# Forward transforms of a graph's tokens from three overlapping blocks of 104 instead of two blocks of 128, and the first filter tiles loaded earlier

## The chip, the cores and the metric

One core of a Trainium2 chip runs the whole program. The metric is the device time of one launch in microseconds (us): the median of three runs of the kernel before is 2039.37 us (2038.85 to 2040.94). Beside these there is one profiled execution, from which all durations below are taken.

The engines are named as in the profile: PE is the matrix engine's matmul side and PEld its weight loads, DVE the vector engine, ACT the scalar engine, POOL the general engine, SP the engine whose queue issues nearly all DMAs.

## The reference, cut to what matters

The input is 64 graphs of 256 nodes (tokens) with 256 features and a 256 x 256 adjacency matrix each, all float32. Two layers follow each other:

```python
# layer 0
h = relu(layernorm(x))
x = x + relu(norm_adj @ h @ W.T + b)
# layer 1
h = relu(layernorm(x))
c = relu(bn1(conv1(h)))              # 1 tap
c = bn2(conv2(c))                    # 17 taps over the tokens, padding 8
x_conv = relu(c + h)
s   = h @ w_se.T + b_se              # 3 columns
A   = exp(-dist(s, s)) * adj
nmp = A @ relu(h @ w_msg.T + b_msg)
gi, gh = [x_conv, nmp] @ w_ih.T + b_ih, h @ w_hh.T + b_hh
r, z = sigmoid(gi_r + gh_r), sigmoid(gi_z + gh_z)
x = x + (1 - z) * tanh(gi_n + r * gh_n) + z * h
```

The change lies in `conv2`, the convolution of 17 taps.

## The kernel before, in words

**The convolution by transforms.** The 256 tokens of a graph are cut into 8 windows. Window `w` has 48 tokens, begins 8 tokens ahead of token 32*w, and yields 32 outputs. Each window is taken to 48 real spectral numbers (`W48`), each spectral number is multiplied by a 256 x 256 filter, and the result is taken back. The 64 graphs go through this in four groups (`GROUPS`) of 16 graphs (`NG`), so that 16 x 8 = 128 windows stand side by side in the tile `Xf` (128 partitions, 48 spectral numbers, two halves of 128 channels, 128 windows).

**The forward transform.** `spectrum(g, cb)` takes one graph and one half of its channels. The graph's tokens lie in the tile `h1l` with tokens on the partitions, as two blocks of 128 tokens. For each block there is one matmul with 128 x 128 of `h1l` as weights and a constant table `dft` as the moving operand. Block 0 holds tokens of windows 0 to 4 and block 1 of windows 3 to 7, so each matmul has 48 x 5 = 240 columns and the two add up in windows 3 and 4. On PE each float32 matmul of the program is two instructions with a weight load each. One `spectrum` is therefore four matmul instructions. Then `act.copy` takes the 384 columns from PSUM into `Xf`.

```python
for nb in range(NB):
    pe.matmul(t[:, :, 3 * nb : 3 * nb + 5], h1[:, nb, cb * P : (cb + 1) * P], dft[:, nb],
              start=(nb == 0), stop=(nb == NB - 1), skip_group_check=True)
```

**Where the tokens come from.** `conv1` writes each graph's `c1o` to a scratch in device memory, `h1d`, as it lies in the tile (each partition's two rows of 1 KB next to each other, 2 KB), and `h1_load` brings it back into `h1l`. There are three buffers of `h1l` (`H1 = 3`): when the second half of graph g is done, the load for graph g + 3 is issued from SP's queue.

**The products.** `product(u)` multiplies spectral unit u (24 of them) by its filters. The filters come from the scratch `wfd` in 71 parts of 256 KB, through six buffers `wf` (`WF = 6`): `wf_load(n)` loads part n, and each part's use issues the load of the part six further on.

**The order of the work.** The first stage computes layer 0, `conv1` and the messages for all graphs, in a loop over `n`; the group 0 of the convolution (16 x 2 calls of `spectrum`, then 24 of `product`) is dealt out between its matmuls. Then comes, for q = 1, 2, 3, a stage of its own with the 32 calls of `spectrum` of group q back to back, here called the spectrum stage of group q; after it the loop over the 16 graphs of group q - 1 calls `gates`, with the products of group q dealt out between the gates of the first four graphs. At q = 4 only gates are left. PE, ACT, DVE and POOL instructions of this part keep the order in which they are written; `after(beats, go)` puts off a step by so many calls of `beat`, and `Paced` deals out the inverse transforms by the time that `beat` is told. In the spectrum stage each `spectrum` ends with `cv.beat(0.81)`.

In the stage of group q the first six filter parts are loaded at its last six graphs: `if g >= NG - WF: wf_load(g - NG + WF)`.

Of the kernel before, what the change touches and what calls it, by code (L numbers as in the profile page):

```python
# [11 lines left out]
FP = mybir.dt.float32  # L12
# [15 lines left out]
W48 = 48  # L28
OUT = 32
# [7 lines left out]
    return 2.0 * np.pi * f / W48  # L37


def dft_table():  # L40


    tab = np.zeros((128, 2, W48, 5), np.float64)
    p = np.arange(128)
    for b in range(2):
        for k in range(5):
            w = 128 * b + p - (OUT * (3 * b + k) - 8)
            inside = (w >= 0) & (w < W48)
            tab[:, b, 0, k] = inside / 48.0
            tab[:, b, 1, k] = inside * (1.0 - 2.0 * (w % 2)) / 48.0  # L50
            for u, f in enumerate(CPLX, 1):
                a = turn_of(f) * (w % W48)
                tab[:, b, 2 * u, k] = inside * np.cos(a) / 24.0
                tab[:, b, 2 * u + 1, k] = inside * -np.sin(a) / 24.0
    return tab.astype(np.float32)


def filter_table():
# [127 lines left out]
def gnn_kernel(  # L186
# [9 lines left out]
    nc = tc.nc  # L196
    B, N, D = x.shape
    P = 128
    KW = conv2_w.shape[2]
    NB = N // P  # L200
# [3 lines left out]
    NG = 16  # L204
    WT = N // OUT
    GROUPS = B // NG
# [4 lines left out]
    def scratch(name, shape):  # L211
        return dram.tile(shape, FP, tag=name, name=name)
# [2 lines left out]
    h2_d = [scratch(f"h2d_{q}", [NG * N, D]) for q in range(GROUPS)]  # L215
    hT_d = [scratch(f"hTd_{g}", [P, DC * N]) for g in range(B)]
    xn_d = [scratch(f"xnd_{g}", [P, DC * N]) for g in range(B)]
    h1_d = [scratch(f"h1d_{g}", [P, NB * D]) for g in range(B)]

    wt_d = scratch("wtd", [KW, D, D])  # L220
    wf_d = scratch("wfd", [3 * UNITS, D, D])
# [12 lines left out]
    brzB = const.tile([P, 2 * D], FP, tag="brzB", name="brzB")  # L234
    bnB = const.tile([P, 2 * D], FP, tag="bnB", name="bnB")

    dft = const.tile([P, 2, W48, 5], FP, tag="dft", name="dft")

# [33 lines left out]
    H1 = 3  # L274
# [10 lines left out]
    def conv_begin(q):  # L285
        cv.q = q
        cv.free = [[Z(cv.scr, 2 * k), Z(cv.scr, 2 * k + 2)] for k in (2, 4)]
        cv.G, cv.A, cv.y, cv.at = {}, {}, {}, {}

    def h1_load(q, g):  # L290
        h1 = cv.stream.tile([P, NB, D], FP, tag="h1l", name=f"h1l_{q}_{g}", bufs=H1)
        cv.dma.dma_start(h1, h1_d[q * NG + g].rearrange("p (c d) -> p c d", c=NB))
        cv.h1[q, g] = h1

    def spectrum(g, cb):

        q, Xf, h1 = cv.q, cv.Xf, cv.h1[cv.q, g]
        t = cv.bank(f"df_{q}_{g}_{cb}")[:, : W48 * WT].rearrange("p (s w) -> p s w", s=W48)
        for nb in range(NB):
            pe.matmul(  # L300
                t[:, :, 3 * nb : 3 * nb + 5], h1[:, nb, cb * P : (cb + 1) * P], dft[:, nb],
                start=(nb == 0), stop=(nb == NB - 1), skip_group_check=True,
            )
        if cb == DC - 1:
            del cv.h1[q, g]
            if g + H1 < NG:
                h1_load(q, g + H1)
        after(0, lambda: act.copy(Xf[:, :, cb, g * WT : (g + 1) * WT], t))
        cv.beat(0.81)

    def sums(u):

# [8 lines left out]
    def wf_load(n):  # L321
        if n < len(PARTS):
            u, k = PARTS[n]
            cv.wf[n] = wf = cv.stream.tile(
                [P, DC, D], FP, tag="wf", name=f"wf_{cv.q}_{u}_{k}", bufs=WF
            )
            cv.dma.dma_start(wf, wf_d[3 * u + k].rearrange("(c p) d -> p c d", c=DC))
# [236 lines left out]
    with ExitStack() as one:  # L564
# [483 lines left out]
        def conv1(g):  # L1048
            t = to_rows(g, "c1", w1T)

            def keep():
                h1 = work.tile([P, NB, D], FP, tag="c1", name=f"c1o_{g}")
                act.activation(h1, t, AF.Relu)
                nc.sync.dma_start(h1_d[g].rearrange("p (c d) -> p c d", c=NB), h1)
            after(1, keep)
            if g + 1 < B:
                after(2, lambda: own_bank("c1", g + 1, b1B))
# [244 lines left out]
        begin()  # L1302
        for n in range(4, B + 5):
            even, odd = n % G == 0, n % G == 1
            if n == B + 1:
                early_stack.close()
                kept()
                for g in range(H1):
                    h1_load(1, g)
            elif n == B + 2:  # L1310
                paced.do(4, outputs_out)
            if filtering and not items:
                filtering.clear()
                while due:
                    beat(0.0)
                conv_start()
            if n == B - 2:

                share[:] = 0.45, 0.6, 0.33
            elif n == B:  # L1320
                share[:] = 0.65, 0.75, 0.4
            if even and n + 2 * G < B:
                load(n + 2 * G)
            if n <= B + 1:
                turn_h(n - 2)
            beat(0.4)
            item()
            if n < B:
                aggregate(n)
                if odd and n + 1 < B:  # L1330
                    after(2, lambda n=n: factors(n + 1))
                    for r in range(NR):
                        after((5, 7, 8, 9)[r], lambda r=r, n=n: layer0_in(n + 1, (r,)))
                if even and n < B - G:
                    for r in (0, 2):
                        after(1 + r // 2, lambda r=r, n=n: row_moments(n + G, (r, r + 1)))
                if even and n + G < B:
                    after(4, lambda n=n: degrees(n + G))
            beat(1.7)
            item()  # L1340
            if even and n <= B + 2:
                turn_cols(n - 4)
            beat(0.2)
            if n + 1 < B:
                turn_adj(n + 1)
            beat(0.4)
            item()
            if n >= 5:
                pass_messages(n - 5)
            beat(1.7)  # L1350
            item(True)
            if n <= B + 1:
                messages(n - 2)
            beat(1.7)
            item()
            if even and n <= B + 2:
                distance(n - 4)
            beat(0.6)
            item()
            if n < B:  # L1360
                project(n)
            beat(1.7)
            item(True)
            if n <= B:
                conv1(n - 2)
            elif n == B + 2:
                conv1(B - 1)
            beat(1.7)
            item()
            if later:  # L1370
                for go in later.pop(0):
                    go()
                if not later:
                    while due:
                        beat(0.0)
                    prep_stack.close()
                    spec_stack = ExitStack()
                    spec = spec_stack.enter_context(tc.tile_pool(name="spec", bufs=1))
                    tab = spec.tile([P, 3 * UNITS], FP, tag="tab", name="tab")
                    nc.sync.dma_start(tab, nc.inline_tensor(filter_table(), name="tab_c").ap())  # L1380
                    tp = {k: filter_load(k) for k in range(2)}
                    filtering.append(True)
                    pace[:] = FILTER / 2, -7.0
                    items.extend(
                        lambda k=k, j=j: filter_part(k, j) for k in range(4) for j in range(QC // 8)
                    )
# [249 lines left out]
    for q in range(1, GROUPS + 1):  # L1636
        share[:] = 0.6, 0.6, 0.3
        ld = gate_inputs(q - 1, 0)
        paced.drain()
        outputs_out()  # L1640
        paced.drain()
        cv.taken = 0
        if q == 1:
            gate_weights()
        first = dict(zip((1, 3, 5, 6), gate_parts(ld, xcT)))
        todo = []
        if q < GROUPS:
            conv_begin(q)
            for g in range(NG):
                if g >= NG - WF:  # L1650
                    wf_load(g - NG + WF)
                for cb in range(DC):
                    spectrum(g, cb)
                if g in first:
                    first.pop(g)()
            while paced.lines[2]:
                beat(0.2)
            for u in range(1, AHEAD):
                sums(u)
            todo = [lambda u=u: product(u) for u in range(UNITS)]  # L1660
        for go in first.values():
            go()
        for g in range(NG):
            share[:] = (0.44, 0.58, 0.3) if todo else (0.53, 0.66, 0.3)
            lead = [todo.pop(0) for _ in range(LEAD if todo and g == 0 else 0)]
            between = [todo.pop(0) if todo else lambda: None for _ in range(PER)]
            ahead, nxt = None, None
            if g + 1 < NG:
                ahead = gate_inputs(q - 1, g + 1)
                nxt = gate_parts(ahead, xcT)  # L1670
            gates(ld, lead, between, nxt)
            ld = ahead
            if q + 1 < GROUPS and g >= NG - H1:
                h1_load(q + 1, g - NG + H1)
    while due:
# [33 lines left out]
```

## Time and profile before

| | |
|---|---|
| median of three runs | 2039.37 us (2038.85 to 2040.94) |
| the profiled execution | 2038.4 us, of which 2036.6 us from its first to its last instruction |
| granted clock of PE | 0.997 |
| busy: PE, PEld, DVE, ACT, POOL | 98%, 85%, 69%, 50%, 54% |
| `df` matmuls (the forward transforms) | 512 instructions, 111.6 us busy |
| spectrum stages of groups 1, 2, 3 | from 837.9, 1158.5 and 1479.2 us, some 28 us each |
| forward transforms of group 0 | between 370 and 474 us, among other matmuls |
| DMA queue that SP feeds | 329.62 MB, 51.3% of the 16 DMA engines' time |

How to read it: a group's line gives the line of the program, the engine, the operation, the tile it writes and those it reads, the shape, the number of instructions; then the busy time in us and the mean ns of one; then the idle time of the engine just ahead of them and what ended it. Nearly all instructions carry L102, the line of a helper that records them, so groups are told apart by tiles. Matmuls are pipelined: an instruction's own duration is longer than its step to the next one. In the timeline a row gives the start, the length, the engine, the group and a count, and in brackets the idle time ahead of it with its releaser.

### The profile page before, as it was taken

What the parts mean: (1) busy time and instruction counts of PE and PEld (TensorE: products, weight loads), DVE (VectorE), ACT (ScalarE), POOL (GpSimd) and SP (SyncE); (2) the same over time, 40 slices, a digit from 0 to 9 for tenths busy, and PEclk for the clock granted to TensorE, in tenths of its full rate; (3) what the DMA queues carried; (4) which work ended last, traced back from release to release, by engine and by line L of the source; (5) the groups of instructions that cost most, each with busy time, mean ns of one, the idle gap of its engine ahead of it and who ended that gap; (6) DMA issues with size and microseconds to landing.
All of it is one profiled execution on the core that took longest, in us unless ns stands there. A gap on an engine that the chain in (4) does not pass through costs nothing. (4 is left out here: it accounts for less than half of the span.)

```text
span 2036.6 us, 33041 instructions
## 1 busy us (share of the span) xinstructions
PE 1998.3 (98%) x10857; PEld 1738.0 (85%) x10857; DVE 1402.9 (69%) x3182; ACT 1013.4 (50%) x2203; POOL 1104.6 (54%) x1298
## 2 busy tenths in 40 slices
PE   7999999999999999899999999999999999999998
PEld 6877777888998888799888899888889988888887
DVE  5657666544488888337999825999924999965555
ACT  5757666665446777523344532344443244443333
POOL 4333333334775554358666528676627776655544
PEclk9999999999999999999999999999999999999999
DMA  8797887656755553666223366433266532223222
GB/s 287 253 249 258 242 254 249 226 168 221 241 182 191 169 175 139 209 194 205 93 94 100 111 209 197 125 99 95 93 195 205 155 99 89 93 86 101 93 88 73
DMA packets 283279, 336.17 MB, mean 165 GB/s; under 512 B 18499, under 2 KB 231126, under 8 KB 282454
## 3 DMA queue, kind: packets, MB, share of 16 engines
q1 hardware_dynamic: 282822, 329.62, 51.3%
q0 software_dynamic: 288, 4.46, 0.6%
q8 instruction: 87, 1.43, 0.3%
q14 instruction: 82, 0.67, 0.1%
HBM read 207.65 MB, written 126.35 MB: 164 GB/s over the span
## 5 line engine op out<-in xcount | busy, mean ns | idle before, releaser
L102 PE MATMUL n<-wiT,hx 128*128 128x256 f32 x1024 | 241.9, 379 | 0.0
L102 PEld LDWEIGHTS n<-wiT,hx 128*128 128x128 f32 x1024 | 194.6, 190 | 26.5
L102 DVE SCALAR_TENSOR_TENSOR Xf<-Xf 128x256 f32<-128x256 f32 (+1 forms) x248 | 182.6, 755 | 14.0 <-ACT Xf L102 10.3
L102 PEld LDWEIGHTS y<-Xf,wf 128*128 128x128 f32 x1536 | 184.7, 192 | 8.2 <-PE tc L102 2.8
L102 PE MATMUL y<-Xf,wf 128*128 128x128 f32 x1536 | 186.7, 275 | 3.1 <-issue 3.1
L102 PE MATMUL ta<-T,S 128*128 128x256 f32 x768 | 186.8, 379 | 1.7 <-ACT p L102 1.7
L102 POOL TENSOR_TENSOR rs<-ve,mhalf 128x2 f32<-128x2 f32 x65 | 52.2, 803 | 230.9 <-DVE nm L102 229.8
L102 PEld LDWEIGHTS ta<-T,S 128*128 128x128 f32 x768 | 144.2, 190 | 20.8 <-ACT p L102 2.1
L102 POOL TENSOR_TENSOR rz<-u,p 128x256 f32<-128x256 f32 x64 | 48.7, 761 | 201.9 <-ACT u L102 187.3
L102 DVE TENSOR_TENSOR Xf<-y,k 128x256 f32<-128x256 f32 x184 | 69.3, 418 | 127.1 <-PE y L102 99.1
L102 POOL TENSOR_TENSOR xs<-Xf 128x256 f32<-128x256 f32 x92 | 70.3, 770 | 151.2 <-PE y L102 103.1
L102 ACT ACTIVATE rz<-rz 128x512 f32<-128x512 f32 x128 | 80.1, 626 | 120.7 <-DVE rz L102 112.7
L102 DVE SCALAR_TENSOR_TENSOR h2l<-rz,h2l 128x256 f32<-128x256 f32 x128 | 107.3, 839 | 44.4 <-POOL h2l L102 44.4
L102 POOL TENSOR_TENSOR aT<-e,adjT 128x512 f32<-128x512 f32 x62 | 83.4, 1362 | 99.5 <-ACT e L102 95.6
L102 POOL TENSOR_TENSOR Xf<-Xf 128x256 f32<-128x256 f32 (+2 forms) x136 | 130.2, 963 | 3.4 <-DVE Xf L102 1.4
L102 ACT COPY k<-y 128x512 f32<-128x512 f32 x92 | 53.9, 586 | 156.7 <-PE y L102 156.7
L102 PE MATMUL n<-whT,hx 128*128 128x256 f32 x512 | 131.4, 379 | 0.0
L102 PE MATMUL ms<-wmT,h2T 128*128 128x259 f32 x512 | 126.6, 390 | 4.4 <-ACT h2T L102 4.4
L102 POOL TENSOR_TENSOR adjH<-adjT,eye 128x512 f32<-128x512 f32 x63 | 82.4, 1307 | 85.4 <-ACT adjT L102 84.1
L102 PE MATMUL ag<-adjH,hs 128*128 128x256 f32 x512 | 124.0, 384 | 3.2 <-ACT hs L102 2.3
L102 PE MATMUL nm<-aT,mso 128*128 128x256 f32 x512 | 122.1, 382 | 4.8 <-DVE pre L102 3.5
L102 PE MATMUL o<-w0T,aggT 128*128 128x256 f32 x512 | 124.0, 385 | 1.1 <-ACT e L102 1.1
(178 smaller groups left out, 5032.6 us busy)
## 6 DMA issues: line engine op xcount, KB each, us to landing
wf<-wfd SPq DMA_DIRECT2D x284, 256.0 KB
wfd<-fo SPq DMA_DIRECT2D x32, 576.0 KB
x2d<-x SPq DMA_DIRECT2D x64, 256.0 KB
h2d<-h SPq DMA_DIRECT2D x64, 256.0 KB
hTd<-h2T SPq DMA_DIRECT2D x64, 256.0 KB
h1d<-c1o SPq DMA_DIRECT2D x64, 256.0 KB
xnd<-xnT SPq DMA_DIRECT2D x64, 256.0 KB
h1l<-h1d SPq DMA_DIRECT2D x64, 256.0 KB
```

What stands on the lines that cost most here:

```text
L102: return self.tc.keep_in_program_order(getattr(self.engine, op)(*args, **kwargs))
```

## The change

The tokens of a graph are read as three blocks of 104 tokens that begin at tokens 0, 76 and 152. Block 0 holds the windows 0 to 2 whole, block 1 the windows 3 and 4, block 2 the windows 5 to 7. Each half of a graph takes three matmuls with 144, 96 and 144 columns, none of which adds to another. `h1d` now has one row of 1 KB for each token; it is stored as such, and `h1_load` reads 104 partitions x 3 rows of 1 KB out of it with steps that overlap (312 KB instead of 256 KB). The table `dft` has 384 columns instead of 480. `beat` is told 0.71 instead of 0.81. The first six filter parts of group 1 are loaded in the first stage (`n == B - 2`; that queue is ordered by a scheduler, which puts them right behind the last filter loads of group 0), and those of groups 2 and 3 one each behind the gates of graphs 8 to 13 of the group before.

```diff
+CHUNK, SHIFT = 104, 76
+SPANS = ((0, 3), (3, 5), (5, 8))
...
-    h1_d = [scratch(f"h1d_{g}", [P, NB * D]) for g in range(B)]
+    h1_d = [scratch(f"h1d_{g}", [N, D]) for g in range(B)]
...
-    dft = const.tile([P, 2, W48, 5], FP, tag="dft", name="dft")
+    dft = const.tile([P, W48 * WT], FP, tag="dft", name="dft")
...
+    def overlapped(rows):
+        return bass.AP(
+            tensor=rows.tensor, offset=rows.offset,
+            ap=[[D, CHUNK], [SHIFT * D, len(SPANS)], [1, D]],
+        )
     def h1_load(q, g):
-        h1 = cv.stream.tile([P, NB, D], FP, tag="h1l", name=f"h1l_{q}_{g}", bufs=H1)
-        cv.dma.dma_start(h1, h1_d[q * NG + g].rearrange("p (c d) -> p c d", c=NB))
+        h1 = cv.stream.tile([P, len(SPANS), D], FP, tag="h1l", name=f"h1l_{q}_{g}", bufs=H1)
+        cv.dma.dma_start(h1[:CHUNK], overlapped(h1_d[q * NG + g]))
...
-        for nb in range(NB):
+        for c, (w0, w1) in enumerate(SPANS):
             pe.matmul(
-                t[:, :, 3 * nb : 3 * nb + 5], h1[:, nb, cb * P : (cb + 1) * P], dft[:, nb],
-                start=(nb == 0), stop=(nb == NB - 1), skip_group_check=True,
+                t[:, :, w0:w1], h1[:CHUNK, c, cb * P : (cb + 1) * P],
+                dft[:CHUNK, W48 * w0 : W48 * w1].rearrange("p (s w) -> p s w", s=W48),
+                start=True, stop=True, skip_group_check=True,
             )
...
-        cv.beat(0.81)
+        cv.beat(0.71)
...
-                nc.sync.dma_start(h1_d[g].rearrange("p (c d) -> p c d", c=NB), h1)
+                nc.sync.dma_start(h1_d[g].rearrange("(c p) d -> p c d", p=P), h1)
...
+            if n == B - 2:
+                for k in range(WF):
+                    wf_load(k)
...
-                if g >= NG - WF:
-                    wf_load(g - NG + WF)
...
+            if q + 1 < GROUPS and 8 <= g < 8 + WF:
+                wf_load(g - 8)
```

More of the change, by code (lines that the diff above doesn't have):

```diff
@@ L37, in turn_of @@
     return 2.0 * np.pi * f / W48
+CHUNK, SHIFT = 104, 76
+SPANS = ((0, 3), (3, 5), (5, 8))
 def dft_table():
-    tab = np.zeros((128, 2, W48, 5), np.float64)
+    tabs = []
     p = np.arange(128)
[L45 to L50, printed above, removed]
+    for c, (w0, w1) in enumerate(SPANS):
+        tab = np.zeros((128, W48, w1 - w0), np.float64)
+        for k in range(w1 - w0):
+            w = SHIFT * c + p - (OUT * (w0 + k) - 8)
+            inside = (w >= 0) & (w < W48) & (p < CHUNK)
+            tab[:, 0, k] = inside / 48.0
+            tab[:, 1, k] = inside * (1.0 - 2.0 * (w % 2)) / 48.0
             for u, f in enumerate(CPLX, 1):
                 a = turn_of(f) * (w % W48)
-                tab[:, b, 2 * u, k] = inside * np.cos(a) / 24.0
-                tab[:, b, 2 * u + 1, k] = inside * -np.sin(a) / 24.0
-    return tab.astype(np.float32)
+                tab[:, 2 * u, k] = inside * np.cos(a) / 24.0
+                tab[:, 2 * u + 1, k] = inside * -np.sin(a) / 24.0
+        tabs.append(tab.reshape(128, -1))
+    return np.concatenate(tabs, 1).astype(np.float32)
 def filter_table():
@@ L298, in spectrum @@
         t = cv.bank(f"df_{q}_{g}_{cb}")[:, : W48 * WT].rearrange("p (s w) -> p s w", s=W48)
-        for nb in range(NB):
+        for c, (w0, w1) in enumerate(SPANS):
             pe.matmul(
-                t[:, :, 3 * nb : 3 * nb + 5], h1[:, nb, cb * P : (cb + 1) * P], dft[:, nb],
-                start=(nb == 0), stop=(nb == NB - 1), skip_group_check=True,
+                t[:, :, w0:w1], h1[:CHUNK, c, cb * P : (cb + 1) * P],
+                dft[:CHUNK, W48 * w0 : W48 * w1].rearrange("p (s w) -> p s w", s=W48),
+                start=True, stop=True, skip_group_check=True,
             )
```

## The prediction

> **What bounds the kernel now.** I read the page first, then the groups by form, then timelines of the stages that the change touches, and last the DMA semaphores in the trace.
>
> ```profile
> span 2036.6 us, 33041 instructions
> PE 1998.3 (98%) x10857; PEld 1738.0 (85%) x10857; DVE 1402.9 (69%) x3182; ACT 1013.4 (50%) x2203; POOL 1104.6 (54%) x1298
> ```
>
> PE is busy throughout; what shortens PE's stream shortens the span where nothing else becomes late. The groups give the work that is changed:
>
> ```profile
> L102 PE MATMUL y<-Xf,wf 128*128 128x128 f32 x1536 | 186.7, 275 | 3.1 <-issue 3.1
> L102 PE MATMUL df<-dft,h1l 128*128 128x240 f32 x512 | 111.6, 368 | 4.0 <-DMA h1l<-h1d 3.1 <-ACT Xf L102 0.9
> L102 ACT COPY Xf<-df 128x384 f32<-128x384 f32 x128 | 60.9, 480 | 40.9 <-PE df L102 40.3
> ```
>
> The `df` matmuls already waited 3.1 us for `h1l`, the load that the change makes larger. PE's timelines give the steps (first in group 0, then in the stage of group 1, then a product):
>
> ```profile
> 370.00 0.97 PE L102 MATMUL df<-dft,h1l 128*128 128x240 f32 x4
> 370.81 1.89 PE L102 MATMUL o<-w0T,aggT 128*128 128x256 f32 x8
> ...
> 854.75 5.63 PE L102 MATMUL df<-dft,h1l 128*128 128x240 f32 x27
> 860.80 2.77 PE L102 MATMUL df<-dft,h1l 128*128 128x240 f32 x12 [0.42 <-DMA h1l<-h1d]
> ...
> 882.15 1.95 PE L102 MATMUL y<-Xf,wf 128*128 128x128 f32 x16
> ```
>
> A row's length less one matmul's own duration, over the steps in it: 240 columns take (5.63 - 0.37) / 26 = 202.5 ns, 256 columns (1.89 - 0.38) / 7 = 216, 128 columns with a weight load for each (1.95 - 0.275) / 15 = 111.7. The line through the first two is 0.84 ns a column and 1.5 ns: 144 columns would take 122 ns, 96 columns 82.
>
> **The matmuls.** Each half of a graph had four steps of 202.5 ns, 810 ns. Now it has four of 122 and two of 96 columns. No row shows a matmul so short. Its lower end is the line, 82 ns. The upper end is the product row, 112 ns: there each step carries a weight load of 128 columns, and 128 columns by the line would be 109, so the load, not the matmul, seems to end the step. The trace has two loads of `df` that nothing held apart, at 860.773 and 860.882 us: 109 ns. I take 112, since a load must fit beside each short matmul: 4 x 122 + 2 x 112 = 712 ns, or 98 ns saved a half (158 ns at the lower end). A graph takes 1.42 us instead of 1.62.
>
> The Trainium skill bears against the change here: "TensorE: Matmul & The Clock Gate", section "LDWEIGHTS (loading the stationary operand)", says that a weight load's time goes by its columns over 1.2 and not by its rows, so 104 rows would load no faster than 128. By it the short step would be about 107 ns, an estimate, and the half 702 ns.
>
> **Group 0.** Between 370 and 474 us the `df` matmuls stand among others with PE busy all the time (the windows give 104.00 of 104.00 us), a graph passes every 6.5 us, so a slower load is hidden. 32 halves x 98 ns = 3.1 us gained (5.1 at the other end).
>
> **The load.** In the stages of groups 1 to 3 the load for graph g + 3 is issued when graph g is done and must have landed two graphs later: 2 x 1.62 = 3.24 us before, 2 x 1.42 = 2.84 after. What must fit: in the trace PE's next graph began at 856.98 and SP issued at 857.18 (0.20); the load landed 3.49 us after its issue, at 860.67; the next weight load began at 860.77 (0.10), and the restart cost another 0.10. Sum 3.89, less 3.24 is 0.65 lost, and the matmul starts show just that. So the chain is 0.40 us plus the landing time.
>
> Undisturbed, the semaphores show landing times of 2.5 to 2.8 us, say 2.6. A load of 128 partitions raises its semaphore by 16 separate landings: 16 engines with 8 packets of 2 KB (median 84 ns). The number of engines goes by partitions: the 72-partition stores `wfd<-fo` show one raise 0.48 us after the issue, before data can have landed, and then 12; a 3-partition load shows one and 3. So 104 = 8 x 13 partitions should go to 13 engines, with 8 x 3 = 24 packets of 1 KB (median 46 ns, mean 52). Transfer 24 x 46 = 1.10 us against 8 x 84 = 0.67: 0.43 later, 3.03 us. The filter loads, 16 packets of 1 KB an engine, landed at best in 2.52, and 8 packets more make 2.9. Ends: 2.8 (19.5 packets on 16 engines) and 3.4 (the excess of the means under load). Chain 3.43 against 2.84: about 0.59 lost, once in three graphs, because three buffers go round together. A graph in the load-bound rhythm costs 1.42 + 0.20 = 1.62, as before: in these stages the wait takes back most of what PE gains.
>
> The skill's "DMA: Bandwidth & Descriptors", section "Why a DMA increments its semaphore by 16 and not by 1", has a rule for it: the largest number up to 16 that divides the slowest dimension. It gives 13 too, so the sum by it is the same; but the page's section "Rules for kernel authors" asks for a multiple of 16 there, which speaks against blocks of 104.
>
> **Group 1's stage** now runs from 837.89 to 865.85. SP is held by the `hx` loads until 840.29, and the first `h1l` load behind them landed at 843.81. With 0.43 more graph 3 starts at 844.37, later than the 843.95 before: the first three graphs gain nothing. With 0.1 for the restart and 13 graphs x 1.42 = 18.5 it would end at 862.9; four waits of 0.59 make 865.3. Gain 0.5. Before, the filter loads in the last six graphs put 0.9 us into the loads' landing (3.5 us each of the last three); that is gone.
>
> **Groups 2 and 3** open with another wait:
>
> ```profile
> 1160.44 0.47 ACT L102 COPY Xf<-df 128x384 f32<-128x384 f32 x1
> 1161.77 0.42 ACT L102 ACTIVATE nn<-u 128x256 f32<-128x256 f32 x1 [0.86 <-DVE u L102]
> 1162.09 0.58 ACT L102 COPY n<-bnB 128x512 f32<-128x512 f32 x1
> 1162.61 1.23 ACT L102 COPY Xf<-df 128x384 f32<-128x384 f32 x3
> ...
> 1163.13 7.56 PE L102 MATMUL df<-dft,h1l 128*128 128x240 f32 x36 [0.45 <-ACT Xf L102]
> ```
>
> ACT is held by the last gates' chain, three PSUM banks are full, and PE stands after 2.5 graphs until 1163.13. ACT's and DVE's order is the same in both programs, so this time stays. From it 13.5 graphs x 1.42 = 19.2, four waits 2.4, 0.1 restart and 0.2 for a load that meets the output store make 1185.0 against 1186.6: 1.6 gained. Group 3, from 1483.89 to 1507.13, likewise 1.4.
>
> **The filter loads.** In the compared order of SP's queue, group 1's six follow group 0's last one among the stores of `h1d`, `hTd` and `h2d`, ahead of `xnd`. They wait for the products to release `wf`; by PE's timeline the last such matmuls end at 599.9 us, `xnd` was issued at 602.41: nothing behind them is late. If it were, a store would slip by up to 4 us, and its tile has two buffers. The other twelve wait for nothing (the products end at graph 3) and cost SP 0.36 us each, while the DMA engines are 30% busy; `hx` is needed a whole graph later. The first product waited for no DMA before, so earlier filters bring nothing there. The `h1d` stores have twice the packets of half the time: nothing. ACT copies at 480 ns fit into 712, and the smaller beat reorders one POOL subtraction.
>
> **The sum.** 3.1 + 0.5 + 1.6 + 1.4 = 6.6 us. The profiled execution took 2038.4 us, the median 2039.37 is 1.0 above it; so 2031.8 and, for the median, 2032.7.
>
> **Rivals.** *The load stays hidden*: chain at or under 2.84, landing under 2.45. The 13 waits (three stages of four, and group 1's graph 3) of about 0.59 would be gone: 7.5 more, 2025.2. Against it: no load landed under 2.47 even with 16 KB an engine. Chance 0.15. *Loaded packets*: the landing time rises to 3.6, as the last three loads of a stage showed, at every load; 13 x 0.57 = 7.4 is lost again and the time is about 2040. The 13 engines would be 78% busy (1.10 of 1.42 us) where 16 were 41% busy (0.67 of 1.62). Chance 0.15. *Slower, by the number of engines*: if the load went to 8 engines, 104 = 8 x 13, an engine would have 39 packets, 39 x 52 = 2.0 us a graph and a stage 3 x 1.42 + 13 x 2.0 = 30.3 against 28.0; three times 2.3 less 3.1 is 3.8 lost, 2043.2, and more with waits on top. It decides from 1.9 us a load upwards. The 72-partition store, on 12 engines and not 8 or 9, speaks against. Chance 0.08.
>
> **The numbers.** My forecast has 0.62, with its own range 2029 to 2036.5 by landing times of 2.8 to 3.3. 0.2%, about what a measurement of this kernel can tell from no change, is 4.1 us, so faster means under 2035.3: 0.55 of the forecast and the hidden case, 0.70. Same: the forecast's upper end 0.07, most of the loaded case 0.13, 0.20. Slower: 0.10. The range 2026.5 to 2038.5 leaves out the 8 engines, half the loaded case and part of the hidden one.
>
> **What would show it.** Right: `df` steps of 122 and 112 ns, 712 ns a half, in group 0 without waits; in the stages a wait of PE for `h1l` of some 0.6 us every third graph, 24 packets of 1 KB an engine and 13 landings a load, stages of about 27.4, 26.5 and 26.5 us. Wrong: stages near 23 us (the load hidden), steps of 82 ns, or stages over 28 us.

## The result, and the profile after

The changed kernel takes 2045.28 us (median, 2043.07 to 2056.19) where the kernel before takes 2039.87 us (2036.39 to 2042.85) on the same chips, 20 runs each. The ratio is 1.0035 with a 95% interval of 1.0025 to 1.0045: 5.4 us slower by the medians and 7 us by the ratio, where 6.6 us faster was forecast. The profiled execution took 2047.6 us, at a mean granted clock of 0.992 against 0.997 before.

The head of its page (the first two lines) and the groups of the forward transforms, from the groups by form (busy us, mean ns, then PE's idle time ahead of them and what ended it):

```profile
span 2045.8 us, 33539 instructions
PE 1998.9 (98%) x11113; PEld 1742.9 (85%) x11113; DVE 1401.8 (69%) x3182; ACT 1012.7 (50%) x2203; POOL 1104.4 (54%) x1298
```

```profile
L108 PE MATMUL df<-dft,h1l 104*128 104x144 f32 x512 | 106.0, 314 | 12.6 <-DMA h1l<-h1d 8.5 <-ACT Xf L108 3.7
...
L108 PE MATMUL df<-dft,h1l 104*128 104x96 f32 x256 | 48.4, 273 | 0.0
```

PE is as busy as before, 1998.9 against 1998.3 us, though it has a fifth fewer `df` columns, and the span is 9.2 us longer. The busy times of the two groups overlap and do not add up. Together the `df` matmuls keep PE busy for 111.5 us, as long as before (111.6), where the kernel without the loads, shown below, needs 97.9 us for the same ones: their durations stretch when the clock falls. The wait for `h1l` has grown from 3.1 to 8.5 us. The windows show where the time went (stages of groups 1, 2 and 3, then the first stage's part with group 0; columns as the first line tells), first for the kernel before, then for the changed one:

```profile
core 0: us, PE busy (x) PEld busy (x) DVE busy (x) ACT busy (x) POOL busy (x), PEclk, DMA share, GB/s
837.90:865.90 28.00, 26.66 (x133) 24.22 (x130) 1.56 (x2) 16.82 (x36) 11.57 (x15) 1.00 0.69 209
1158.40:1186.60 28.20, 26.73 (x131) 24.06 (x129) 7.42 (x18) 16.33 (x35) 5.30 (x6) 1.00 0.63 193
1479.20:1507.20 28.00, 26.77 (x130) 24.11 (x130) 7.38 (x18) 16.33 (x35) 5.28 (x6) 1.00 0.65 194
370.00:473.80 103.80, 103.80 (x545) 90.92 (x544) 51.19 (x172) 66.77 (x141) 35.02 (x45) 1.00 0.59 193
```

```profile
core 0: us, PE busy (x) PEld busy (x) DVE busy (x) ACT busy (x) POOL busy (x), PEclk, DMA share, GB/s
835.60:869.50 33.90, 30.01 (x197) 28.43 (x194) 1.11 (x2) 16.84 (x36) 11.60 (x15) 0.85 0.57 160
1162.00:1191.50 29.50, 24.93 (x195) 23.39 (x194) 7.45 (x18) 16.33 (x35) 5.33 (x6) 1.00 0.61 173
1484.10:1516.40 32.30, 28.16 (x194) 26.63 (x193) 7.39 (x18) 16.33 (x35) 5.27 (x6) 0.89 0.56 158
369.40:470.50 101.10, 101.10 (x610) 90.00 (x609) 51.16 (x172) 65.78 (x141) 34.80 (x45) 1.00 0.65 210
```

From the starts of PE's instructions the stages take 33.8, 29.4 and 32.3 us against 28.0, 28.1 and 27.9 before: 11.5 us lost. The part of group 0 takes 101.0 against 103.8: 2.8 us gained. The remaining 0.5 us up to the 9.2 lies ahead of and between these parts. PE's timeline of the stage of group 1:

```profile
835.62 4.67 PE L108 MATMUL df<-dft,h1l 104*128 104x144 f32 x36
842.50 15.45 PE L108 MATMUL df<-dft,h1l 104*128 104x144 f32 x84 [2.20 <-DMA h1l<-h1d]
858.94 1.67 PE L108 MATMUL df<-dft,h1l 104*128 104x144 f32 x12 [1.00 <-DMA h1l<-h1d]
860.78 6.75 PE L108 MATMUL df<-dft,h1l 104*128 104x144 f32 x48 [0.17 <-DMA h1l<-h1d]
867.93 1.67 PE L108 MATMUL df<-dft,h1l 104*128 104x144 f32 x12 [0.40 <-DMA h1l<-h1d]
```

The first three graphs (36 instructions) pass in 4.4 us, then PE stands 2.20 us. After that 84 instructions take 15.45 us, 184 ns each instead of some 120. Two things are seen here: PE waits for the load, and a stretch runs slowly. The windows of the two stretches of the stages with the lowest granted clock (same columns) tell why:

```profile
844.20:854.40 10.20, 10.20 (x44) 10.20 (x45) 1.11 (x2) 4.01 (x9) 4.73 (x6) 0.50 0.40 109
1496.10:1502.90 6.80, 6.80 (x32) 6.80 (x31) 0.00 (x0) 2.08 (x5) 0.00 (x0) 0.50 0.51 127
```

PE's clock was granted at half, 0.50, for 10.2 and 6.8 us. The steps there are 240 ns for 144 columns. The kernel before has no such stretch between 151 and 2035 us. The changed kernel has one more, 3.4 us from 823.7 us, ahead of the stages and behind a wait of PE for DVE; the kernel without the loads, shown below, has it too, so it does not come from them.

### The profile page after: what moved, and what is told of

It reads as the page before. It is cut to its first block, busy times and chain, and to the rows that moved or that the text cites. A ratio compares the mean times of both kernels' runs of the same rounds, so it can differ in the third digit from the quotient of the medians.

```text
span 2045.8 us, 33539 instructions
## 1 busy us (share of the span) xinstructions
PE 1998.9 (98%) x11113; PEld 1742.9 (85%) x11113; DVE 1401.8 (69%) x3182; ACT 1012.7 (50%) x2203; POOL 1104.4 (54%) x1298
```

## The experiments

Two theories were set against each other. Theory A: the `h1l` load lands too late for three buffers, PE waits, and the waits bring the clock down. The rivals: the moved filter loads cost time elsewhere (B), the new matmuls are slow in themselves (C), the size of the load or of its rows counts (D, E). Ratios below are against the kernel before on the same chip, with 95% intervals; times are medians.

### The filter loads alone, and the change without them

`wf_alone` is the kernel before with this edit only; `wf_back` is the changed kernel with it undone:

```diff
+            if n == B - 2:
+                for k in range(WF):
+                    wf_load(k)
...
-                if g >= NG - WF:
-                    wf_load(g - NG + WF)
...
+            if q + 1 < GROUPS and 8 <= g < 8 + WF:
+                wf_load(g - 8)
```

> The kernel before with the filter loads moved as in the change, transforms as before. Theory A (late h1l loads and the clock that drops while PE waits make the loss): the last three h1l loads of a stage land 2.6 us after issue instead of 3.5, some 0.7 us a stage, so 2 to 2.5 us faster than before, about 2037.5. Theory B (the moved filter loads cost time elsewhere): 3 us or more slower than before.

> The changed kernel with the filter loads back in the last six graphs of the stage. Theory A: the loads meet the h1l loads, which land later still, 1 to 3 us a stage: 2047 to 2052. Theory B: the loss goes away, 2040 or less.

`wf_alone`: 2038.14 us, 0.9984 (0.9975 to 0.9993). Its stages take 27.3, 27.1 and 27.2 us. `wf_back`: 2059.21 us, 1.0099 (1.0080 to 1.0117), with stages of 35.3, 38.7 and 32.0 us and half clock for 27 us; the loss is larger than expected. Moving the filter loads is therefore a gain of 0.16% by itself and saves the changed kernel some 14 us. Theory B falls.

### The load taken away

`no_load` leaves out the loads of graphs 3 to 15 of each group:

```diff
-    def h1_load(q, g):
+    def h1_load(q, g, old=None):
+        if old is not None:
+            cv.h1[q, g] = old
+            return
...
-                h1_load(q, g + H1)
+                h1_load(q, g + H1, h1)
```

> The changed kernel without the h1l loads of graphs 3 to 15 of each group: these graphs take the tokens of earlier ones, so the output is another; all else as in the change. It takes away the wait for the load alone. Theory A (the load's lateness is the whole loss): stages of 23 to 24 us, no half clock, 2023 to 2027. Theory C (the shorter matmuls are slow or wait for something else): stages stay at 26 us or more, above 2032.

2024.34 us, 0.9919 (0.9903 to 0.9934). PE's timeline of its stage of group 1, and the windows of the three stages (columns as above):

```profile
835.80 23.22 PE L108 MATMUL df<-dft,h1l 104*128 104x144 f32 x192
```

```profile
835.80:858.90 23.10, 23.10 (x197) 23.03 (x194) 1.53 (x2) 16.72 (x36) 12.29 (x15) 1.00 0.18 53
1151.40:1175.50 24.10, 23.15 (x194) 22.91 (x193) 7.53 (x18) 16.32 (x35) 5.42 (x6) 1.00 0.13 42
1468.10:1492.20 24.10, 23.14 (x194) 22.90 (x194) 7.42 (x18) 16.33 (x35) 5.29 (x6) 1.00 0.12 39
```

All 192 instructions of the stage of group 1 run without a gap, 23.05 us for 32 halves, 720 ns each, at full clock. The stages of groups 2 and 3 take 24.05 us each, with a single wait of some 0.95 us, for ACT. So nothing is wrong with the matmuls (C falls), and the loads cost the changed kernel 2045.28 - 2024.34 = 20.9 us by the medians, and 1.16% or some 24 us by the ratios. In the profiled executions the loss lies in the stages alone: the three together differ by 24.4 us, the spans by 24.0.

### More buffers, or a larger block

`h1_4` has `H1 = 4`. `c112` has other blocks, which also hold the windows whole, and 112 = 7 x 16 partitions; `c128` likewise with 128. `c112_h4` has both.

```diff
-    H1 = 3
+    H1 = 4
```

```diff
-CHUNK, SHIFT = 104, 76
+CHUNK, SHIFT = 112, 72      # c112, c112_h4;  128, 64 in c128
```

> The changed kernel with four buffers of h1l instead of three: a load has three graphs, 3 x 1.42 = 4.27 us, from issue to use. Theory A: chain 0.4 + 3.3 to 3.9, nearly all waits go and the clock stays up: stages of 23 to 25 us instead of 29 to 34, 2023 to 2029. Theory C: the stages stay as long as in the change, 2043 or more.

> Three blocks of 112 tokens at 0, 72, 144: 112 partitions are 16 x 7, so 16 engines with 21 packets of 1 KB instead of 13 with 24; matmul columns as in the change. Theory A: the loads land about 0.3 to 0.5 us earlier (near 3.0 to 3.2), waits of PE some 0.4 us shorter 13 times and less or no time at half clock: 2032 to 2039. Theory C (the matmuls of 104 rows are slow themselves): steps stay at 240 ns in part of the stages, 2045. Theory D (the size of the load counts, not the engines): no earlier landing, 2045.

> Three blocks of 128 tokens at 0, 64, 128: 16 engines with 24 packets of 1 KB, 384 KB a load; matmul columns as in the change. If the number of packets an engine counts, the loads land as in the change (3.3 us alone) and the time is that of the change, 2043 to 2048. If the bytes of the whole load count, they land later than there and the time is 2048 or more. If engines count more than packets, near the version with 112 tokens, 2040 to 2043.

> Blocks of 112 tokens (16 engines) and four buffers of h1l. Theory A: the load has 4.27 us and the chain is 0.4 + 3.0 to 3.7, so most waits go: stages of 23.5 to 25.5 us, 2025 to 2030, some 4 us below the version with 104 tokens and four buffers. Rival (with four loads on their way the DMA engines set the pace, whatever their number): no better than that version, 2032.

| kernel | engines x packets a load | landing alone, us | landing in the stages, us (median) | time, us | ratio |
|---|---|---|---|---|---|
| before | 16 x 8 of 2 KB | 2.58 | 2.74 | | |
| the change | 13 x 24 of 1 KB | 3.43 | 3.70 | 2045.28 | 1.0035 (1.0025 to 1.0045) |
| `h1_4` | 13 x 24 | 3.39 | 4.23 | 2032.61 | 0.9964 (0.9951 to 0.9976) |
| `c112` | 16 x 21 | 2.90 | 3.68 | 2040.83 | 1.0001 (0.9991 to 1.0011) |
| `c128` | 16 x 24 | 3.07 | 3.56 | 2041.82 | 1.0002 (0.9991 to 1.0012) |
| `c112_h4` | 16 x 21 | 2.94 | 4.04 | 2028.35 | 0.9948 (0.9933 to 0.9962) |

Landings are from the semaphores in the traces, from the issue to the last raise; "alone" is the median of the faster half of the last 16 loads of group 0, which are 6.5 us apart. Windows of the stages of `h1_4`, then of `c112_h4` (columns as above):

```profile
834.80:862.30 27.50, 25.01 (x196) 23.42 (x193) 2.01 (x2) 16.83 (x36) 11.93 (x15) 1.00 0.77 185
1154.90:1181.60 26.70, 24.10 (x194) 23.12 (x194) 7.41 (x18) 16.33 (x35) 5.29 (x6) 1.00 0.64 179
1474.20:1500.80 26.60, 24.57 (x193) 23.36 (x192) 7.39 (x18) 16.33 (x35) 5.26 (x6) 1.00 0.70 179
```

```profile
835.50:860.40 24.90, 23.78 (x196) 23.14 (x193) 2.01 (x2) 16.80 (x36) 11.92 (x15) 1.00 0.80 216
1153.10:1178.30 25.20, 23.65 (x194) 23.03 (x193) 7.33 (x18) 16.31 (x35) 5.19 (x6) 1.00 0.70 198
1471.00:1496.60 25.60, 23.99 (x194) 23.13 (x193) 7.38 (x18) 16.30 (x35) 5.25 (x6) 1.00 0.73 197
```

The fourth buffer gives back most of the loss and all of the clock in the stages, though each load then lands later. But `h1_4`, expected at 2023 to 2029, missed: between 842 and 851 us its 1 KB packets took 78 ns on the mean and a load landed every 1.7 us, so there the loads themselves set the pace:

```profile
842.00:851.00 9.00, 8.89 (x66) 7.96 (x66) 1.98 (x2) 4.79 (x10) 6.33 (x8) 1.00 0.92 191
```

A DMA share of 0.92 with 191 GB/s; the stage of `c112_h4` moves 216 GB/s at 0.80. Sixteen engines bring stages near those without the load. `c112_h4` beats both kernels. `c128`, with more bytes and the same number of packets an engine, lands 0.36 us earlier than the change when alone and is 0.33% faster against the common base, so for the landing the number of engines counts, not the bytes (D falls). `c112` came in above its expectation by 2 us: alone its loads land 0.53 us earlier, but in the stages hardly, and its profiled execution has stages of 34.5, 29.8 and 30.0 us. What delays its loads there was not settled. How 16 engines make `c112` and `c128` faster is not shown either. In the profiled executions the stage of group 2, at full clock in all of them, takes 29.8 (`c112`) and 29.9 us (`c128`), no less than the 29.4 of the change. But none of their 22 executions has a mean clock under 0.994, where 7 of the 20 of the change have.

### The same bytes on 16 engines, and rows of 1 KB

`split96` cuts each load of the changed kernel in two. `rows1k` is the kernel before with `h1d` in rows of 1 KB.

```diff
-        cv.dma.dma_start(h1[:CHUNK], overlapped(h1_d[q * NG + g]))
+        for p0, p1 in ((0, 96), (96, CHUNK)):
+            cv.dma.dma_start(h1[p0:p1], overlapped(h1_d[q * NG + g], p0, p1))
```

```diff
-    h1_d = [scratch(f"h1d_{g}", [P, NB * D]) for g in range(B)]
+    h1_d = [scratch(f"h1d_{g}", [N, D]) for g in range(B)]
...
-        cv.dma.dma_start(h1, h1_d[q * NG + g].rearrange("p (c d) -> p c d", c=NB))
+        cv.dma.dma_start(h1, h1_d[q * NG + g].rearrange("(c p) d -> p c d", p=P))
...
-                nc.sync.dma_start(h1_d[g].rearrange("p (c d) -> p c d", c=NB), h1)
+                nc.sync.dma_start(h1_d[g].rearrange("(c p) d -> p c d", p=P), h1)
```

> The changed kernel with each h1l load cut in two DMAs, of 96 partitions (16 engines with 18 packets) and of 8 partitions (8 engines with 3 more): the same 312 KB, but on 16 engines with at most 21 packets each. Theory A (13 engines are a part of the lateness): landing alone near 2.9 us as with 112 tokens instead of 3.4, time near that version, 2039 to 2043. Rival (the second issue costs as much as it gains, or engines do not matter): 2044 to 2049.

> The kernel before with h1d in rows of 1 KB for each token: the same 256 KB on 16 engines, as 16 packets of 1 KB instead of 8 of 2 KB. Theory A (bytes and engines count, not the row): landing 2.5 to 2.8 us, time within 2 us of before. Theory E (rows of 1 KB are slow in themselves): landing 0.3 us or more later and PE waits, 3 us or more slower.

`split96`: 2039.40 us, 0.9999 (0.9990 to 1.0009). With the same 312 KB and one more issue for each load, the loss against the kernel before is gone: the two parts together land 3.37 us after the first issue (median in the stages) instead of 3.70. Alone they land after 3.38 us, hardly before the 3.43 of the change, so that part of the expectation (2.9) missed. Nor is the earlier landing the whole gain: in the profiled executions the stage of group 1, with 10.2 us at half clock in both, takes 33.2 us instead of 33.8, and that of group 2, at full clock in both, 28.8 instead of 29.4. More comes from the stage of group 3, 28.4 instead of 32.3 us, where only the change has half clock, and 3.5 us from the time ahead of the first transform of group 0, where the two kernels hardly differ. `rows1k`: 2041.58 us, 0.9998 (0.9987 to 1.0009), landing alone 2.67, in the stages 2.84. Rows of 1 KB cost 0.1 us of landing and no time; E falls.

### PE kept at work in its waits

`warm` puts matmuls that nobody reads into the waits:

```diff
             for g in range(NG):
+                if g >= H1 and g % H1 == 0:
+                    for k in range(1 + (g == H1)):
+                        t = cv.bank(f"warm_{q}_{g}_{k}")
+                        pe.matmul(t, ident, brzB, start=True, stop=True)
                 for cb in range(DC):
                     spectrum(g, cb)
```

> The changed kernel with one matmul of 512 columns (two instructions, about 0.86 us) that nobody reads ahead of graphs 3, 6, 9, 12 and 15 of each stage, two of them ahead of graph 3, so that PE works in a part of its waits; some 5 us of extra matmul time a stage. Theory A1 (the clock drop is a good part of the loss, and idle PE brings it): no stretch at half clock, stages of groups 1 and 3 come down by 2 to 5 us, 2038 to 2043. Theory A2 (waiting alone is the loss, the clock does not matter since the load sets the pace): no faster than the change, 2045 to 2050.

2048.72 us, 1.0039 (1.0026 to 1.0051), and still half clock for 3.4 and 6.8 us in the stages. The time agrees with the expectation's A2, but the experiment decides nothing: the clock fell all the same, and the extra work cost its own time. The price of the clock is read better from the 20 runs of the changed kernel, each with its mean clock: 13 with a clock of 0.994 or more took 2044.67 us (median), 7 at 0.990 to 0.992 took 2050.39. Read so, the waits alone make the kernel about 5 us slower than before, and in a third of the executions the lower clock goes with some 6 us more; no experiment took the clock alone away.

### The scratch laid out for the load

`packed` stores what a partition loads as one row of 3 KB, with blocks of 112; `packed_h4` adds `H1 = 4`.

```diff
-    h1_d = [scratch(f"h1d_{g}", [N, D]) for g in range(B)]
+    h1_d = [scratch(f"h1d_{g}", [CHUNK, len(SPANS) * D]) for g in range(B)]
...
-                nc.sync.dma_start(h1_d[g].rearrange("(c p) d -> p c d", p=P), h1)
+                for c in range(len(SPANS)):
+                    for nb in range(NB):
+                        lo = SHIFT * c
+                        t0, t1 = max(lo, nb * P), min(lo + CHUNK, (nb + 1) * P)
+                        if t0 < t1:
+                            nc.sync.dma_start(
+                                h1_d[g][t0 - lo : t1 - lo, c * D : (c + 1) * D],
+                                h1[t0 - nb * P : t1 - nb * P, nb],
+                            )
```

> h1d holds 112 rows of 3 KB: each partition's three tokens stand next to each other, conv1 stores them with four DMAs a graph, and a load is 112 partitions x 3 KB, 16 engines with 7 packets of 3 KB; three buffers. Theory A (packets on an engine set the landing): 7 x 0.12 = 0.85 us a load, landing 2.75 alone and 3.0 to 3.3 in the stages; waits of 0.5 to 0.9 us 13 times: 2031 to 2037. Rival (the four stores hold up SP's queue in the first stage): stages shorter but the first one 3 us or more longer, 2038 or more.

> The packed scratch and four buffers of h1l. Theory A: the load is hidden, stages of 23 to 24.5 us as without the load, 2024 to 2028, the best of all. Rival (stores in the first stage): 2030 or more.

`packed`: 2043.47 us, 1.0020 (1.0010 to 1.0029), a miss: seven packets of 3 KB (121 ns median, but 154 to 158 on the mean in the stages) land after 3.04 us alone and 3.43 in the stages, no better than 21 of 1 KB when alone. Its stages take 28.7, 28.5 and 29.2 us, somewhat longer than before. The rival, a first stage longer by 3 us, does not show in the profile: the stage of group 1 begins at 836.8 us, 1.2 us later than in the change. `packed_h4`: 2030.21 us, 0.9950 (0.9936 to 0.9964), stages of 24.8, 25.0 and 25.0 us: 2 us above its expectation, and the same as `c112_h4` within the intervals. The layout buys nothing over 16 engines and a fourth buffer.

## Why the prediction was wrong

**The matmuls were right.** Group 0, as the first row of a half and what follows it shows, starts the next matmul 0.71 us later, where four steps of before took 0.81:

```profile
369.42 0.88 PE L108 MATMUL df<-dft,h1l 104*128 104x144 f32 x6
370.13 1.89 PE L108 MATMUL o<-w0T,aggT 128*128 128x256 f32 x8
```

712 ns were forecast, 720 are measured without the load, and group 0 gained 2.8 us of the 3.1. On the mean the short steps were held near the 112 ns of the product row (720 less four of 122 leaves 116 for each), and not near 82. Single starts in `no_load`'s stage of group 1 show how: behind the first matmul of 96 columns the next one starts after 83 ns, but the two that follow after 112 and 152 ns, while the weight loads there are 110 to 112 ns apart. The Trainium skill's "TensorE: Matmul & The Clock Gate", section "LDWEIGHTS (loading the stationary operand)", led to expect a bound by the weight load; the estimate of 107 ns from it was a little low.

**The lead of the load was right, the rhythm of the waits was not.** A load is issued when its graph is done and is needed two graphs later, as forecast; the rival in which the load stays hidden was put at 2025.2 us, and without the load the kernel takes 2024.34. But "once in three graphs" is not what the timelines show. PE's rows in the stage of group 2, at full clock throughout (12 instructions are a graph):

```profile
1162.05 3.73 PE L108 MATMUL df<-dft,h1l 104*128 104x144 f32 x30
1166.77 3.93 PE L108 MATMUL df<-dft,h1l 104*128 104x144 f32 x30 [0.98 <-ACT Xf L108]
1171.37 3.46 PE L108 MATMUL df<-dft,h1l 104*128 104x144 f32 x24 [0.67 <-DMA h1l<-h1d]
1175.35 4.59 PE L108 MATMUL df<-dft,h1l 104*128 104x144 f32 x36 [0.51 <-ACT Xf L108]
1180.84 3.27 PE L108 MATMUL df<-dft,h1l 104*128 104x144 f32 x24 [0.91 <-DMA h1l<-h1d]
1184.30 1.67 PE L108 MATMUL df<-dft,h1l 104*128 104x144 f32 x12 [0.19 <-DMA h1l<-h1d]
1187.14 4.52 PE L108 MATMUL df<-dft,h1l 104*128 104x144 f32 x36 [1.17 <-DMA h1l<-h1d]
```

Behind the first row break, which is the forecast wait for ACT, PE stands ahead of graphs 5, 7, 10, 12 and 13 (graph 7's load landed at 1175.21 us, just ahead of its row). These waits and their restarts make the stage 5.4 us longer than without the loads (29.44 against 24.05), where the prediction charged 2.4 for them.

**The term that was mis-sized is the landing time.** The step "Chain 3.43 against 2.84" took 3.03 us for it, with ends of 2.8 and 3.4. Measured are 3.43 us alone and 3.70 in the stages (median; the mean is 3.88). With 3.70 the same sum reads: chain 0.40 + 3.70 = 4.10, lead 2 x 1.44 = 2.88, 1.2 us lost 13 times, 16 us; with the mean 18 us. The runs give 2044.67 - 2024.34 = 20.3 us for executions with a high clock, where the forecast had 7.5; the 2 to 4 us left over are not accounted for. Two errors are seen in the term. The packets were priced at the median of 46 ns for the quiet transfer, where in the changed kernel's stages they took 56 to 59 ns on the mean. And 13 engines were counted as costing only their longer share: the 3.03 us are about what 24 packets take alone on each of 16 engines (3.07, `c128`), and on each of 13 they land 0.36 us later. The 13 engines themselves were foreseen, and the traces show 13 landings after one early raise.

**The rule against 104 was cited and not weighed.** The advice of a multiple of 16 in the Trainium skill's "DMA: Bandwidth & Descriptors", section "Rules for kernel authors", stood in the prediction with no price. `split96` gives one: 0.36% between the two ratios, of which only a part is the earlier landing, as said there.

**A cost was left out.** No rival had the clock. PE's clock was high throughout the stages of before, and nothing in the prediction asked what a PE that waits up to 2.2 us does to it. In the profiled execution 17.0 us of the stages ran at half clock.

**The filter loads** cost nothing where they were put, as forecast, and gained somewhat more than the prediction named.

**The chances.** "Loaded packets", at about 2040 us and with 0.15, was the rival nearest to the event, and even it had the landing at 3.6 us and a waiting time of 15 us. The slower rival had 8 engines, which the trace does not show.

## What to carry to other kernels

Where a load and its use form a ring of few buffers, shortening the work shortens the load's time as well: work out issue to landing against (buffers - 1) times the new step, with the landing times that a loaded queue shows and not the quiet ones, before counting the gain. Add the buffer with the shorter step: here a fourth one turned +0.35% into -0.36%, and blocks of 112 tokens on top into -0.52%. When an engine's idle time grows, look at the granted clock of the stretch, since a wait may cost more than its length.

## What the runs showed of the hardware that was not expected

- Half clock after short waits. The granted clock in the traces changes only on a fixed grid of 3.41 us, and its fall goes with PE's idle time within one step of the grid, not with the length of a wait. Over the 14 profiled executions, without their first 100 and last 20 us, all 20 steps at full clock in which PE stood 2.0 us or more (by the profile's ends of the matmuls) were followed by half clock; of the steps with 1.37 to 1.99 us 6 were and 14 were not; of those with less none was. `c112` shows both (columns as above): its wait of 2.63 us falls into the first two steps and leaves the clock alone, its shorter one of 2.35 us falls into the third step nearly whole, and the fourth runs at half clock.

```profile
835.10:838.50 3.40, 2.38 (x19) 2.17 (x18) 0.00 (x0) 2.13 (x5) 3.01 (x5) 1.00 0.82 264
838.50:841.90 3.40, 1.79 (x15) 1.82 (x16) 0.00 (x0) 0.56 (x2) 2.70 (x4) 1.00 0.76 180
848.80:852.20 3.40, 1.10 (x9) 0.88 (x8) 0.00 (x0) 0.96 (x2) 0.15 (x1) 1.00 0.68 207
852.20:855.60 3.40, 3.35 (x14) 3.38 (x15) 0.00 (x0) 0.68 (x2) 0.00 (x0) 0.50 0.03 11
```

In the stages half clock lasted one to three steps, 3.4 to 10.2 us; in the stage of group 1 above it stayed although PE was busy for 10.20 of the 10.20 us. What sets that number is not shown.

- Engines. A load of 104 partitions goes to 13 engines, and with the same 24 packets an engine it lands 0.36 us later than one of 128 partitions on 16, which is larger. With four loads on their way on 13 engines (`h1_4`, 842 to 851 us) the packets took 78 ns.
- Packets. On 16 engines alone, 16, 21 and 24 packets of 1 KB land in 2.67, 2.90 and 3.07 us: some 0.05 us for each packet.
- Filter loads of 256 KB among the `h1l` loads took the changed kernel from 2045 to 2059 us, far more than the 3 us that moving them gave the kernel before. A part of it is the clock: 27 us of its profiled execution ran at half.
